# A two-layer graph network in fp32: four batches together through layer 1, its adjacency products in two Strassen levels

## The chip, the cores and the metric

The kernel runs on one core of one Trainium2 chip. The metric is the device time of one execution in microseconds (us), a median over several executions. All data is fp32.

The engines are named as in the profile: PE (TensorE, matmuls), PEld (its weight loads), DVE (VectorE), ACT (ScalarE), POOL (GpSimd), SP (SyncE, which here only issues DMAs). A matmul multiplies a stationary operand of at most 128 by 128 (loaded first) with a moving operand of up to 512 columns, and leaves the result in one of eight PSUM banks, each of 512 fp32 columns over 128 partitions. ACT and DVE bring results from there into SBUF.

## What is computed

The input `x` has 32 batches of 512 nodes by 128 features; `adj` is 512 by 512.

```
# layer 0: x, adj x, adj^2 x, adj^3 x, mixed by weights (adj is given twice, so pairs of weights add up)
y_1 = einsum('bnik,iok->bno', x_all, weight_1)
x = layernorm(x + y_1)
# layer 1: five gated steps on h, starting from h = x
m_in = m_out = einsum('nm,bmd->bnd', adj, h)
u3 = h @ u3_w.T + u3_b
z  = sigmoid(av @ w3_w.T + w3_b + u3)
r  = sigmoid(av @ w4_w.T + w4_b + u3)
hv = tanh(av @ w5_w.T + w5_b + (r * h @ u5_w.T + u5_b))
h  = (1 - z) * h + z * hv
x = layernorm(x + h)
```

Since both halves of `av` are the same m = adj h, each gate weight is the sum of its two halves: one 128 by 128 matrix each (`w3s`, `w4s`, `w5s`).

## The kernel before, in words

**Tiling.** A node is (partition, k) with k from 0 to 3, so an array of one batch is four chunks of 128 by 128. The 32 batches are 16 pairs. `pair(q, key0)` (L1035) takes a pair through `layer0` (L701) and then through five steps. `h` is kept feature-major (`hT`, 128 features by 512 nodes); the adj product needs it node-major (`X`). `turn` (L345) makes one from the other: a DVE transposition of 32 by 32 blocks (L360), four DMAs to a buffer `d` in HBM (L352) and one back (L358).

**The adj product of a step.** `pair_product` (L514) multiplies the pair's two batches, side by side, with adj as a 2 by 2 block product in Winograd's form of Strassen: POOL makes sums of the input blocks (L511) and PE makes 7 half-products for 8, each of two matmuls of 256 columns (L524). `seven` (L393) arranges them for both kinds of product. It uses three banks, `a`, `b` and `c`: products 1, 3, 5 and 6 accumulate one after the other in bank `a`, and between them ACT copies the sum so far (L385), since each intermediate sum is itself wanted; so product 3 must wait for the copy after product 1, and so on. DVE adds what else belongs together (L389).

**The two-level form** exists already for the `adj x` of layer 0: from the third pair on, two pairs (four batches) go through `quad_product` (L565), which splits each block again: 49 quarter products for 64, each one matmul of 128 columns (L628). It is done in two runs of `seven`: half A, whose seven groups hold four quarter products each, and half B, whose seven groups hold three. In B, DVE adds A's result while it takes the product out of PSUM (L386), and further sums are made by DVE (L685).

**The gates of a step**, one batch at a time (`gates`, L901, matmuls of 512 columns in L909): w4·m into bank `pr`, w3·m into `pz`, w5·m plus u5·(r h) into `ph`. u3·h goes into a bank of its own (L1049), ACT moves it to SBUF with its bias (L1054), and DVE adds it to `pr` (L915) and `pz` (L922) ahead of the sigmoids (L917, L924). L918 makes r h, L956 the tanh, L970 and L972 make z (hv - h), and POOL adds that to h (L974).

**Layer 0 after the product**: weights (L766), the product with adj squared (L831), a layer norm (`norm`, L304: moments on DVE, L313 and L314; the power -1/2 and small steps on POOL, L317 to L322; the application on ACT, L330). **The end**: the last pairs' last steps transpose on PE, and the last pair ends in halves (`last_finish`, L977).

**What sets the order.** No queue is filled in program order: `Plan` (L47) is a list scheduler that runs when the program is built. Each operation has an engine, an assumed duration, what it comes after, buffers it takes and gives back (`slots`, L157) and a key; the ready operation with the lowest key goes next on its engine. `KEYS` (L24) and `LONG` (L25) are keys of the pairs and the distance of steps. The order of instructions on each engine is then fixed in the program.

Of the kernel before, what the change touches and what calls it, by code (L numbers as in the profile page):

```python
# [9 lines left out]
F32 = mybir.dt.float32  # L10
# [4 lines left out]
P = 128  # L15
NK = 4
# [6 lines left out]
ON_PE = {14: 2, 15: 2}  # L23
KEYS = [-2.0, 20.0, 50.0, 68.0, 92.0, 118.0, 154.0, 168.0, 186.0, 214.0, 234.0, 268.0, 294.0, 322.0, 346.0, 358.0]  # L24
LONG = 19.0  # L25
# [101 lines left out]
def gnn_resnorm_kernel(  # L127
# [22 lines left out]
    small = ctx.enter_context(tc.tile_pool(name="small", bufs=16))  # L150
# [3 lines left out]
    def tiles(tag, n, shape=(P, N), pool=work):  # L154
# [4 lines left out]
        d=tiles("d", 6, (NR, R, NR, P), dram),  # L159
        hd=tiles("hd", 6, (P, 2, NK, P), dram),  # L160
        xg=tiles("xg", 2, (P, 2, NK, P)),
        xT=tiles("xT", 3),
        M=tiles("M", 1, (P, 4, N)),
        SA=tiles("SA", 1, (P, 25, P)),
        SB=tiles("SB", 1, (P, 15, P)),
        UY=tiles("UY", 2, (P, 4, N)),
        h0=tiles("h0", 4, (P, 2, NK, P)),
        hT=tiles("hT", 8),
        X=tiles("X", 3),
        uT=tiles("uT", 6),  # L170
        rh=tiles("rh", 2),
        z=tiles("z", 3),
        m=tiles("m", 5),
        S=tiles("S", 2, (P, 7, H, P)),
        v=tiles("v", 5),
        two=[None] * 5,
        inside=[None] * 17,
# [9 lines left out]
    mhalf = const.tile([P, 2 * NK], F32, tag="mhalf", name="mhalf")  # L187
# [5 lines left out]
    TT = const.tile([P, 7, 4, P], F32, tag="TT", name="TT")  # L193
    make_identity(nc, ident)
    nc.vector.memset(mhalf, -0.5)

    def load_x(q, b, engine=nc.sync):
        engine.dma_start(plan[f"xg{q}"][:, b], x[2 * q + b].rearrange("(p k) c -> p k c", k=NK))

    def loaded_x(q, key):  # L200

        take = [("xg", f"xg{q}")]
        first = plan("SP", 0.42, lambda: load_x(q, 0), take=take, key=key, late=4.5)
        return first, plan("SP", 0.42, lambda: load_x(q, 1), after=[first], key=key, late=4.5)

    def second_x(after):

        emit = lambda b: load_x(1, b, nc.scalar)
        after = after + [place]
        first = plan("ACT", 0.45, lambda: emit(0), after=after, key=-60.0, late=3.2)  # L210
        return first, plan("ACT", 0.45, lambda: emit(1), after=after, key=-60.0, late=3.2)
# [6 lines left out]
    def first_x():  # L218
        emit = lambda: load_x(0, 0)
        a = plan("SP", 0.42, emit, take=[("xg", "xg0")], key=-99.0, late=2.9)  # L220
        b = plan("SP", 0.42, lambda: load_x(0, 1), key=-98.0, late=3.4)
        return a, b
# [34 lines left out]
    w0_in = plan("SP", 0.45, lambda: nc.sync.dma_start(w_of(), w0), take=[("UY", "w0")], key=-70.0, late=7.0)  # L257
# [10 lines left out]

    w0_ready = plan("DVE", 2.3, layer0_weights, after=[w0_in], give=[("UY", "w0")], key=-40.0)

    place = plan("-", 0.0, lambda: None, take=[("xg", "xg1")], key=-99.0)
# [5 lines left out]
    def gate_weight(src, name):  # L277
        halves = lambda: plan[name][:, : 2 * P].rearrange("p (h o) -> p h o", h=2)
        w = const.tile([P, P], F32, tag=name, name=name)
# [3 lines left out]
        ready.append(plan("DVE", 0.28, emit, after=[got], give=[("z", name)], key=26.0))  # L283
        return w

    def plain(src, name):
        t = const.tile(list(src.shape), F32, tag=name, name=name)
        ready.append(plan("SP", 0.45, lambda: nc.sync.dma_start(t, src), after=[later], key=23.5, late=4.0))
        return t

    w3s, w4s, w5s = (gate_weight(s, n) for s, n in ((w3, "w3s"), (w4, "w4s"), (w5, "w5s")))
    u3s, u5s = plain(u3, "u3s"), plain(u5, "u5s")
    b3s, b4s, b5s = plain(b3, "b3s"), plain(b4, "b4s"), plain(b5, "b5s")
    ub3s, ub5s = plain(ub3, "ub3s"), plain(ub5, "ub5s")
    hv_b = const.tile([P, 1], F32, tag="hv_b", name="hv_b")
    hv_ready = plan("DVE", 0.1, lambda: nc.vector.tensor_tensor(hv_b, b5s, ub5s, ALU.add), after=ready, key=26.0)
    weights = ready + [hv_ready]
# [6 lines left out]
    def norm(n, name, src_of, dst_of, after, give, key, by_dve=False):  # L304
# [11 lines left out]
        def power():  # L316
            nc.gpsimd.tensor_scalar(rstd, mv[:, :, 1], EPS, None, ALU.add)  # L317
            if not by_dve:
                nc.gpsimd.tensor_scalar(shift, mv[:, :, 0], -1.0, None, ALU.mult)
            nc.gpsimd.tensor_tensor(rstd, rstd, mhalf[:, :n], ALU.pow)  # L320
            if not by_dve:
                nc.gpsimd.tensor_tensor(shift, shift, rstd, ALU.mult)  # L322
# [14 lines left out]
        p = plan("POOL", 1.2 if by_dve else 1.75, power, after=got, key=key)  # L337
# [55 lines left out]
    def seven(name, after, us, terms, product, outs, key, shape, take=(), give=()):  # L393
# [19 lines left out]
        c1 = out(first_out, "a", [p1], 0, 0)  # L413
# [17 lines left out]
    an_of = lambda km: plan[f"an{km // H}"].rearrange("p b k c -> p (b k c)").rearrange("p (k n) -> p k n", k=H)  # L431
    an_ready = []
    for km in range(NK):
        emit = lambda km=km: transposes(plan[f"ba{km}"], lambda k: at[:, k, chunk(km)])
        take = [("bank", f"ba{km}")] + ([("h0", f"an{km // H}")] if km % H == 0 else [])
        tr = plan("PE", 0.44, emit, after=at_in, take=take, key=SQ_KEY)
        emit = lambda km=km: nc.scalar.copy(an_of(km)[:, km % H], plan[f"ba{km}"])
# [3 lines left out]
    an_sum = lambda i: lambda: plan[f"anS{i // H}"][:, i % H].rearrange("p k c -> p (k c)").rearrange(  # L441
        "p (k c) -> p k c", k=H
    )
    sums = []
    for i, (a, b, op) in enumerate(
# [8 lines left out]
        take = [("h0", f"anS{i // H}")] if i % H == 0 else []  # L454
# [26 lines left out]
    give = [("h0", f"{t}{i}") for t in ("an", "anS") for i in range(2)]  # L481
# [32 lines left out]
    def pair_product(X_of, turned, name, dst, S, slots, after, key):  # L514
# [21 lines left out]
        F = lambda i: lambda: fit(S(i), turned)  # L536
        if turned:
            f11 = copied(S_of(4), X11, True, "ACT", [own], key)
            f12 = copied(S_of(5), X12, True, "ACT", [f11], key)
        else:  # L540
            f11 = f12 = own
        s0 = add(0.73, F(0), X21, X22, ALU.add, both, key)
        s1 = add(0.73, F(1), F(0), X11, ALU.subtract, [s0], key)
        s2 = add(0.73, F(2), X11, X21, ALU.subtract, both, key)
        s3 = add(0.73, F(3), X12, F(1), ALU.subtract, [s1], key)
        f22 = copied(S_of(6), X22, True, "POOL", both, key) if turned else own
        L = (S_of(4), S_of(5), S_of(6)) if turned else (X11, X12, X22)
        t = lambda i: lambda: T[:, i]
        terms = [
            (L[0], lambda: B11, [f11, in11]),  # L550
            (L[1], lambda: B21, [f12, in21]),
# [3 lines left out]
            (L[2], t(3), [f22, T_sums[3]] + both),  # L555
# [4 lines left out]
            name, [f11], 0.86, terms, product, into(dst, HN), key, half_bank, give=give  # L560
        )
        read = [s0, s1, s2, s3, f11, f12, f22] if turned else p + [s2, s3]
        return [[e11, e12], [e21, e22]], [read] * 2

    def quad_product(X_of, name, after, key):  # L565
# [3 lines left out]

        SA, SB, PA, M = (f"{t}{name}" for t in ("SA", "SB", "PA", "M"))  # L570
        X = lambda i, j, b: lambda: X_of(2 * i + b)[:, j * H : (j + 1) * H]

        LOW, HIGH = slice(3, 5), slice(5, 7)
        part = lambda S, at, w: lambda: plan[S][:, at + w.start : at + w.stop]

        def inner(S, at, a, after):

            out = lambda i: lambda: plan[S][:, at + i]
            s2 = add(0.45, out(1), a(0, 0), a(1, 0), ALU.subtract, after, key)
            s0 = add(0.45, out(3), a(1, 0), a(1, 1), ALU.add, after, key)  # L580
            s1 = add(0.45, out(0), out(3), a(0, 0), ALU.subtract, [s0], key)
            s3 = add(0.45, out(2), a(0, 1), out(0), ALU.subtract, [s1], key)
            return s1, s2, s3, s0

        quarter = lambda i, j: lambda b, k: lambda: X_of(2 * i + b)[:, j * H + k]
        at_of = {0: 4, 1: 11, 2: 18}

        own = plan("-", 0.0, lambda: None, after=[o for a in after for o in a], take=[("SA", SA), ("UY", PA)], key=key)
        s0, s2, s1 = [], [], []
        for b, w in ((0, HIGH), (1, LOW)):  # L590
            s0.append(add(0.73, part(SA, 11, w), X(1, 0, b), X(1, 1, b), ALU.add, [own], key))
            s2.append(add(0.73, part(SA, 4, w), X(0, 0, b), X(1, 0, b), ALU.subtract, [own], key))
            s1.append(add(0.73, part(SA, 18, w), part(SA, 11, w), X(0, 0, b), ALU.subtract, s0[-1:], key))
        x11 = inner(SA, 0, quarter(0, 0), [own])
        q = lambda i: lambda: plan[SA][:, 4:].rearrange("p (o b) c -> p o b c", o=3)[:, :, i]
        ready = s0 + s1 + s2
        i2 = add(0.98, q(1), q(5), q(3), ALU.subtract, ready, key)
        i0 = add(0.98, q(3), q(3), q(4), ALU.add, [i2], key)
        i1 = add(0.98, q(0), q(3), q(5), ALU.subtract, [i0], key)
        i3 = add(0.98, q(2), q(6), q(0), ALU.subtract, [i1], key)  # L600


        def lefts(S, at, direct):
            sums = {2: 0, 4: 1, 6: 2, 3: 3}
            if direct is None:
                sums = {**sums, 5: 4, 0: 5, 1: 6}
# [579 lines left out]
```

## Time and profile before

| what | us |
| --- | --- |
| median of 3 runs (1510.89 to 1514.23) | 1511.45 |
| span of the profiled execution | 1510.3 |
| PE busy | 1493.2 |
| DVE busy | 1024.4 |
| POOL busy | 848.7 |
| ACT busy | 750.7 |
| the granted TensorE clock, mean | 0.997 of full speed |

The span runs from the first to the last instruction of the profiled execution; the median lies 1.15 us above it. Matmul records overlap: one matmul in fp32 leaves two records, and each is drawn longer than the distance from its start to that of the next[...]. So how long PE needs for a matmul is read from the distance of starts in the timeline, not from the mean of a group. "idle before" in a group's row is the engine's idle time just before such instructions, with the one that ended it.

### The profile page before, as it was taken

Reading aid. Unit: us, or ns where it says so; the run is one execution under the profiler, and the core shown is the slowest. Engines: PE = TensorE matmul, PEld = TensorE weight load, DVE = VectorE, ACT = ScalarE, POOL = GpSimd, SP = SyncE. Lnnn points to the kernel's source line nnn. Section 1 sums busy time; section 2 is a strip of 40 time slices with the busy share of each in tenths; the row PEclk is TensorE's granted clock in tenths of the full one; section 3 lists DMA queues with packets and bytes.
Section 4 is the critical chain, followed back from the end, with each engine's and each line's share of the span. In section 5 each row is a group of like instructions: output and inputs, shape, how many; then the busy total and the mean of one; then the engine's idle time right before and its main releaser. Section 6 shows DMA issues by size and latency. Waiting matters only on the chain.

```text
span 1510.3 us, 21064 instructions
## 1 busy us (share of the span) xinstructions
PE 1493.2 (99%) x6562; PEld 1042.3 (69%) x6562; DVE 1024.4 (68%) x2125; ACT 750.7 (50%) x1584; POOL 848.7 (56%) x1207
## 2 busy tenths in 40 slices
PE   8999999999999999999999999999999999999997
PEld 7877777676667776677676766676766776666665
DVE  6566666767776758667767567768477666766665
ACT  3454444654644644455445445546444455545454
POOL 4856834764544947756367455558464644543454
PEclk9999999999999999999999999999999999999998
DMA  3114423333333433334243242534333332433310
GB/s 110 57 56 112 107 75 92 110 107 84 105 103 107 126 98 93 107 95 119 71 139 90 77 120 92 133 98 126 81 109 92 90 84 70 119 86 89 77 50 28
DMA packets 166176, 142.91 MB, mean 95 GB/s; under 512 B 18992, under 2 KB 128048, under 8 KB 166064
## 3 DMA queue, kind: packets, MB, share of 16 engines
q1 hardware_dynamic: 165776, 141.04, 33.9%
q8 instruction: 52, 0.85, 0.3%
q14 instruction: 60, 0.49, 0.1%
q10 hardware_dynamic: 288, 0.52, 0.1%
HBM read 71.76 MB, written 69.73 MB: 94 GB/s over the span
## 4 chain that ended last, share of the span: by engine, by line
PE 94%; DVE 2%; POOL 1%; issue 1%; DMA 1%; SPq 0%; ACT 0%; POOLq 0%; DVEq 0%
PE bank L909 35%; PE bank L524 32%; PE bank L1049 9%; PE bank L766 6%; PE bank L831 6%; PE bank L628 4%; PE bank L460 1%; PE bank L302 0%; POOL rstd L320 0%; POOL S L511 0%; DVE M L685 0%; DMA at<-in_adjT 0%; DVE UY L685 0%; PE bank L1018 0%; DMA X<-d 0%
## 5 line engine op out<-in xcount | busy, mean ns | idle before, releaser
L974 POOL TENSOR_TENSOR hT<-z,hT 128x512 f32<-128x512 f32 x156 | 199.0, 1281 | 303.9 <-DVE z L972 297.9
L524 PE MATMUL bank<-T,S 128*128 128x256 f32 x1232 | 307.0, 379 | 0.2 <-POOL S L511 0.2
L524 PEld LDWEIGHTS bank<-T,S 128*128 128x128 f32 x1232 | 229.1, 190 | 78.2 <-ACT m L385 28.9
L385 ACT COPY m<-bank 128x256 f32<-128x256 f32 x320 | 119.1, 372 | 277.6 <-PE bank L524 276.5
L524 PE MATMUL bank<-at,S 128*128 128x256 f32 x824 | 211.4, 379 | 0.9 <-ACT S L504 0.6
L389 DVE TENSOR_TENSOR m<-bank,m 128x256 f32<-128x256 f32 x240 | 100.3, 419 | 137.0 <-PE bank L524 94.7
L524 PEld LDWEIGHTS bank<-at,S 128*128 128x128 f32 x824 | 153.7, 190 | 57.3 <-issue 37.3
L970 DVE TENSOR_TENSOR bank<-bank,hT 128x512 f32<-128x512 f32 x156 | 107.8, 694 | 104.4 <-ACT bank L956 103.6
L909 PE MATMUL bank<-rh,u5s 128*128 128x512 f32 (+1 forms) x324 | 159.3, 587 | 0.2 <-ACT bank L936 0.2
L1049 PE MATMUL bank<-hT,u3s 128*128 128x512 f32 x320 | 159.3, 592 | 0.0
L909 PE MATMUL bank<-m,w4s 128*128 128x512 f32 x320 | 158.6, 592 | 0.0
L909 PE MATMUL bank<-m,w3s 128*128 128x512 f32 x320 | 157.0, 592 | 0.0
L909 PE MATMUL bank<-m,w5s 128*128 128x512 f32 x320 | 155.1, 593 | 0.2 <-DVE M L389 0.2
L917 ACT ACTIVATE bank<-bank 128x512 f32<-128x512 f32 x160 | 93.2, 583 | 121.1 <-DVE bank L915 120.7
L1054 ACT ACTIVATE uT<-bank,ub3s 128x512 f32<-128x512 f32 x160 | 109.7, 687 | 83.9 <-PE bank L1049 82.7
L915 DVE SCALAR_TENSOR_TENSOR bank<-bank,b4s,uT 128x512 f32<-128x512 f32 x160 | 119.6, 750 | 46.3 <-PE bank L909 44.1
L956 ACT ACTIVATE bank<-bank,hv_b 128x512 f32<-128x512 f32 x158 | 104.3, 662 | 77.1 <-PE bank L909 76.0
L922 DVE SCALAR_TENSOR_TENSOR bank<-bank,b3s,uT 128x512 f32<-128x512 f32 x160 | 118.9, 750 | 13.8 <-PE bank L909 13.1
L924 ACT ACTIVATE z<-bank 128x512 f32<-128x512 f32 x160 | 95.1, 595 | 59.9 <-DVE bank L922 55.7
L360 DVE STREAM_TRANSPOSE v<-hT 128x512 f32<-128x512 f32 x152 | 105.5, 699 | 20.0 <-POOL hT L974 19.4
L918 DVE TENSOR_TENSOR rh<-bank,hT 128x512 f32<-128x512 f32 x160 | 107.8, 679 | 10.0 <-ACT bank L917 9.2
L972 DVE TENSOR_TENSOR z<-bank,z 128x512 f32<-128x512 f32 x156 | 105.1, 682 | 1.6
(182 smaller groups left out, 2456.1 us busy)
## 6 DMA issues: line engine op xcount, KB each, us to landing
d<-v SPq DMA_DIRECT2D x832, 64.0 KB, 1.8
X<-d SPq DMA_DIRECT2D x152, 256.0 KB, 2.8
v<-d SPq DMA_DIRECT2D x56, 256.0 KB, 2.8
xg<-in_x SPq DMA_DIRECT2D x30, 256.0 KB, 3.0
out<-h SPq DMA_DIRECT2D x30, 256.0 KB, 2.1
hd<-h SPq DMA_DIRECT2D x13, 512.0 KB, 3.8
h<-hd SPq DMA_DIRECT2D x13, 512.0 KB, 3.9
at<-in_adjT SPq DMA_DIRECT2D x4, 256.0 KB, 5.3
```

Source lines behind the costliest of these rows:

```text
L360: blocks = lambda: nc.vector.transpose(plan[f"v{name}"], src_of())
L385: return "ACT", COPY[cols], lambda src: nc.scalar.copy(dst(i, j), src)
L524: nc.tensor.matmul(dst, lhsT=left[:, k, :], rhs=right[:, k, :], start=(first and k == 0), stop=(last and k == H - 1), skip_group_check=True,)
L909: nc.tensor.matmul(plan[dst][:, c], lhsT=w, rhs=plan[src][:, c], start=first, stop=last, skip_group_check=True)
L915: emit = lambda: nc.vector.scalar_tensor_tensor(plan[pr], plan[pr], b4s, plan[uT], ALU.add, ALU.add)
L918: emit = lambda: nc.vector.tensor_tensor(plan[rh], plan[pr], plan[h], ALU.mult)
L922: emit = lambda: nc.vector.scalar_tensor_tensor(plan[pz], plan[pz], b3s, plan[uT], ALU.add, ALU.add)
L970: emit = lambda: nc.vector.tensor_tensor(plan[ph], plan[ph], plan[h], ALU.subtract)
L972: emit = lambda: nc.vector.tensor_tensor(plan[z], plan[ph], plan[z], ALU.mult)
L974: emit = lambda: nc.gpsimd.tensor_tensor(plan[h], plan[z], plan[h], ALU.add)
L1049: emit = lambda bn=bn, hb=h[b]: nc.tensor.matmul(plan[bn], lhsT=u3s, rhs=plan[hb], start=True, stop=True)
L1054: emit = lambda bn=bn, uT=uT: nc.scalar.activation(plan[uT], plan[bn], AF.Identity, bias=ub3s)
```

## The change

Layer 1 takes quads of four batches instead of pairs; `quad(Q, key0)` replaces `pair`, and 8 quads replace 16 pairs.

1. `quad_product` serves the steps too, except those that `PAIRS = {0: (0, 1), 6: (3, 4), 7: (3, 4)}` names (quad: steps), where the new `pair_products` makes two pair products as before. Its input sums are laid out anew (blocks in `SA` and `SB` side by side, so that the inner sums take all blocks at once), copies of plain blocks are made by ACT, and half B adds onto the result of half A in place, all of its seven takings-out on DVE. Of the further sums, three are on DVE and two on POOL.
2. `gates`: u3·h goes straight into `pr`, under w4·m; after the sigmoid of r has read the bank, (w3 - w4)·m is added in the same bank, which makes it the sum for z. So the bank for u3·h, its ACT move and both DVE additions go. m now lies in two pieces of 256 columns, so each of its products is two matmuls. The last addition of h moves from POOL to DVE.
3. `norm`: two of POOL's small steps move to DVE, one goes.
4. Buffers are shared: `E` (5 tiles for four batches each) holds inputs, U and Y, h0, X; `Q` (2) holds m and the layer-0 product; `SB` is one, `SA` two. Every quad's h0 is written to HBM and fetched again at the end. Weights lie in the part of `at` that isn't read any more.
5. The last step of the last quad ends on PE (`finish`), the special endings in halves are gone. All keys are new.

```diff
-ON_PE = {14: 2, 15: 2}
-KEYS = [-2.0, 20.0, 50.0, 68.0, 92.0, 118.0, 154.0, ...]
-LONG = 19.0
+KEYS = [-11.9, 27.7, 78.0, 130.0, 180.1, 230.1, 270.6, 308.3]
+PAIRS = {0: (0, 1), 6: (3, 4), 7: (3, 4)}
+ON_PE = {7: 1}
+LONG = 29.5
...
-        M=tiles("M", 1, (P, 4, N)),
-        SA=tiles("SA", 1, (P, 25, P)),
-        SB=tiles("SB", 1, (P, 15, P)),
+        E=tiles("E", 5, (P, 4, N)),
+        Q=tiles("Q", 2, (P, 5, N)),
+        SA=tiles("SA", 2, (P, 29, P)),
+        SB=tiles("SB", 1, (P, 21, P)),
...
+    emit = lambda: nc.vector.tensor_tensor(w3s, w3s, w4s, ALU.subtract)
...
         def power():
-            nc.gpsimd.tensor_scalar(rstd, mv[:, :, 1], EPS, None, ALU.add)
             nc.gpsimd.tensor_tensor(rstd, rstd, mhalf[:, :n], ALU.pow)
+        def shifts():
+            nc.vector.scalar_tensor_tensor(shift, mv[:, :, 0], -1.0, rstd, ALU.mult, ALU.mult)
...
+    def quad_product(X_of, turned, name, after, key):
+        for b in range(2):
+            f11[b] = copy(blk(SA, 0, b), X(0, 0, b), lo)
+            s0[b] = outer(blk(SA, 2, b), X(1, 0, b), X(1, 1, b), ALU.add, hi)
+            s1[b] = outer(blk(SA, 3, b), blk(SA, 2, b), X(0, 0, b), ALU.subtract, ...)
+            s2[b] = outer(blk(SA, 1, b), X(0, 0, b), X(1, 0, b), ALU.subtract, ...)
+            f12[b] = copy(blk(SB, 0, b), X(0, 1, b), [ownB, *lo])
+            f22[b] = copy(blk(SB, 1, b), X(1, 1, b), [ownB, *hi])
+            s3[b] = outer(blk(SB, 2, b), X(0, 1, b), blk(SA, 3, b), ALU.subtract, ...)
...
+        inA = inner(SA, 1.28, f11 + s0 + s1 + s2)
+        inB = inner(SB, 1.0, f12 + f22 + s3)
...
+        u = sum_of("DVE", 0.8, M_of(3), M_of(3), M_of(0), ends)
+        v = sum_of("POOL", 1.28, M_of(4), M_of(1), M_of(2), ends)
+        e22 = sum_of("POOL", 1.28, M_of(4), M_of(4), M_of(3), [u, v])
...
-            into(dstB, 3 * P, plus),
+            into(dstB, 3 * P, dstB),
+            out_after=[u, v],
...
+        e21 = sum_of("DVE", 0.8, M_of(1), M_of(1), M_of(3), [u] + endsB)
+        e12 = sum_of("DVE", 0.8, M_of(2), M_of(2), M_of(3), [u] + endsB)
...
+    def gates(name, m, h, after, h_in, early, key):
+        emit = lambda: mm(pr, u3s, h, True, False)
+        p = plan("PE", 0.86, emit, after=early + h_in + weights, take=[("bank", pr)], key=key - 0.01)
+        emit = lambda: mm_m(pr, w4s, False, False)
+        p = plan("PE", 0.86, emit, after=after + [p], take=[("bank", ph)], key=key)
+        r = act(ph, pr, AF.Sigmoid, r_b, 0.59, key, [p], take=[("rh", rh)])
+        r2 = dve(rh, ph, h, ALU.mult, key, [r])
+        p2 = plan("PE", 0.86, lambda: mm_m(pr, w3s, False, True), after=[r], key=key + 0.5)
+        zs = act(z, pr, AF.Sigmoid, z_b, 0.59, key + 0.5, [p2], take=[("z", z)], give=[("bank", pr)])
+        p3 = plan("PE", 1.73, candidate, after=[p2, r2], give=[("rh", rh)], key=key + 0.8)
+        t = act(ph, ph, AF.Tanh, hv_b, 0.66, key + 0.8, [p3])
+        t = dve(ph, ph, h, ALU.subtract, key + 0.8, [t])
+        t = dve(ph, ph, z, ALU.mult, key + 0.8, [t, zs], [("z", z)])
+        return p3, dve(h, ph, h, ALU.add, key + 0.8, [t], [("bank", ph)])
...
+    for Q in range(NP // 2):
+        quad(Q, KEYS[Q])
```

In the changed kernel the lines are L662 (quarter products), L747 (pair products of the steps), L1010 and L1014 (gates), L865 and L930 (layer 0), L420 (ACT copies out of PSUM), L421 and L424 (DVE takings-out), L699 (further sums), L602 and L544 (POOL sums), L606 (ACT copies of blocks).

## The prediction

> **What bounds the kernel now.** I read the page's busy times first, then its slices and the chain that ended last, then PE's starts in the timeline, then the windows of the two ends.
>
> ```profile
> PE 1493.2 (99%) x6562; PEld 1042.3 (69%) x6562; DVE 1024.4 (68%) x2125; ACT 750.7 (50%) x1584; POOL 848.7 (56%) x1207
> ...
> PE   8999999999999999999999999999999999999997
> ...
> PE 94%; DVE 2%; POOL 1%; issue 1%; DMA 1%; SPq 0%; ACT 0%; POOLq 0%; DVEq 0%
> ```
>
> PE is busy in 1493.2 of 1510.3 us, full in all slices but the ends, and is 94% of the chain. A busy PE need not be at its peak, so I read the distance of starts (columns: start, length, engine, line, operation, records):
>
> ```profile
> 699.87 1.05 PE L831 MATMUL bank<-S,at 128*128 128x128 f32 x8
> 700.76 1.06 PE L831 MATMUL bank<-UY,at2S 128*128 128x128 f32 x8
> ...
> 706.82 1.89 PE L524 MATMUL bank<-T,S 128*128 128x256 f32 x8
> 708.55 1.02 PE L909 MATMUL bank<-rh,u5s 128*128 128x512 f32 x2
> ...
> 713.71 1.88 PE L909 MATMUL bank<-m,w4s 128*128 128x512 f32 x4
> 715.43 1.88 PE L909 MATMUL bank<-m,w3s 128*128 128x512 f32 x4
> ```
>
> Eight records of 128 columns take 0.89 us, eight of 256 take 1.73, four of 512 take 1.72. At two records each, a matmul costs **0.2225, 0.4325 and 0.86 us**: close to proportional to its columns, 4% dearer per column at 128. The program has 1335, 1180 and 798 of them: 297.0 + 510.4 + 686.3 = 1493.7 us, PE's busy time to 0.5. So the kernel before is PE's columns plus 16.6 us, and these lie at the ends (columns: window, its length, busy us of PE, PEld, DVE, ACT, POOL):
>
> ```profile
> 0.00:10.00 10.00, 5.29 (x16) 4.27 (x17) 0.76 (x2) 2.83 (x4) 3.52 (x10) 1.00 0.62 203
> ...
> 1490.00:1500.00 10.00, 8.83 (x36) 5.16 (x34) 7.37 (x17) 6.79 (x16) 2.01 (x2) 1.00 0.11 44
> 1500.00:1511.00 11.00, 1.90 (x8) 1.45 (x8) 3.73 (x16) 1.51 (x4) 4.86 (x9) 0.59 0.16 56
> ```
>
> 4.7 us are lost at the start and 10.3 at the end. In between, nobody keeps PE waiting: its groups away from the ends show 1 us of idle time at most, while the others wait for it or for each other:
>
> ```profile
> POOL hT L974 <- DVE z L972: 297.9, 97, 18.7
> ACT m L385 <- PE bank L524: 276.5, 266, 5.8
> ```
>
> **What the Trainium skill says.** "TensorE: Matmul & The Clock Gate", part 2, gives N/2.4 + 2.5 ns as the distance of matmuls of N columns, and 55.6 ns measured at 128. A record here is 111 ns at 128 columns and 430 at 512: twice that gap (111 and 432); the trace agrees. "SBUF — State Buffer", "two separate sides": a DVE operation with two SBUF inputs and a GpSimd operation exclude each other for a whole instruction. The trace agrees: L685, both inputs in SBUF, takes 669 ns at best, 744 in the median, 1755 at worst. "PSUM — Partial Sum Buffer", "The four PSUM rules": POOL can't touch PSUM, and a partial sum may be read within an accumulation group. The first is why h's last addition, now from a bank, must be DVE's; `seven` already does the second before.
>
> **The change, part by part.** Counts are from the order of the changed program, which is built but has not run.
>
> *Adj products.* L524's 1148 matmuls of 256 columns become 28 (L557) and 168 (L747): 952 × 0.4325 = 411.7 us less. Quarter products go from 343 to 2009 = 41 × 49 (34 steps, 7 layer-0 products; so the change does what it says): 1666 × 0.2225 = 370.7 more. A quad step costs 49 × 0.2225 = 10.9 us where two pair products cost 28 × 0.4325 = 12.1. **Minus 41.0 us** of PE, on the path.
>
> *Gates.* Still five products for each of 160 batch-steps, but the 480 with m are now two halves: 480 × (0.865 - 0.86) = **plus 2.4**. Sixteen fewer transpositions on PE: **minus 3.6**. The whole: 2985 × 0.2225 + 1184 × 0.4325 + 320 × 0.86 = 664.2 + 512.1 + 275.2 = **1451.5 us, 42.2 less**.
>
> *Other engines*, off the path so long as PE is fed. DVE: out go L915 and L922 (238.5) and 204 of L389 (× 0.419 = 85); in come 160 additions of h × 0.69 = 110, takings-out of quad products 164 × 0.55 + 123 × 0.55 + 123 × 0.685 = 242 less 41 before, 88 more sums of L685's kind at 0.74 to 1.1 = 65 to 97, small norm steps 13: near **1110 us, 75%**. POOL: out go L974 and its like (206), 208 pair sums × 0.74 (154), 50 copies (20), small norm steps (42), the old quad sums (113); in come 328 × 0.74 = 243, 41 × 9.5 = 390 (two of 1.28, six of 1.005, two of 0.46) and 82 × 1.28 = 105: near **1050, 71%**. ACT: minus L1054 (110), minus 272 copies × 0.372 (101), plus 80 and 59 for larger copies: near 680. None passes PE.
>
> *New waits of PE.* In `seven`, product 3 waits for the copy after 1, 5 for that after 3, 6 for that after 5. From the timeline, ACT starts about 0.20 us after PE's next slot, and I add 0.10 for the way back: 0.89 us with a 512-column copy (0.587), 0.67 with a 256-column one (0.372), 0.85 with DVE's 0.55. I laid the matmul costs along the order and measured what PE has to do in between. Half A, 123 such gaps: 5 of zero, 8 of 0.44, 20 of 0.7 to 0.86, falling short by 8.5 us together. B: 0.8 (one of zero, 29 just wide enough). Weights of layer 0: 2.0; pair products: 1.3; from w4 to (w3 - w4), behind the sigmoid: 0.8. Sum **13 us**; the same count before gives about 1. Queued behind the waiting matmul is all of PE. The bound below is zero (a stall in one place widens the next gap), above it twice the sum, when DVE is late.
>
> *Queues and DMA.* From the last candidate of a quad to its next product PE has at least 25 us of other work, in place of the 12 or so of tanh, three DVE operations, transposition, four writes and a fetch: hidden. SP issues 1201 DMAs for 1148, also off the path. Only the last step is tight: 10.3 us for about 12: **plus 2**. At the start the transpositions of the first h0 come 4.4 us of PE work after the product that their norm needs; moments of eight chunks (8 × 0.45), 1.3 for the power and three ACT steps of 0.49 make about 7.5: **plus 3**. After the last matmul group of the gates: tanh 0.66, three DVE steps 2.1, PE 0.9, moments 1.7, power 1.3, four applications 1.4, storing 3.2, and gaps: 12.0 for the 13.5 of before: **minus 1.5**.
>
> *B's first taking-out* waits for u (DVE) and v (POOL), and with it B's third product: after A's last product 0.2, a DVE operation of 0.69, v at 1.28, the taking-out at 0.55 and the ways between, 3.1 us. PE's work in between is 2.0 to 14.5 us; five of 41 places fall short, by 2.4 together. If v stands behind another POOL sum of 1.28 each time, 12.6. I take **4**.
>
> Sum: 1451.5 + 16.6 + 13 + 2 + 3 - 1.5 + 4 = 1488.6 of span; the median stood 1.15 above its span: **1490 us**. What is late next: DVE's queue.
>
> **The rivals.**
> - *As here*, PE bound with 10 to 31 us of new waits: 1479 to 1500, chance 0.62.
> - *PE filled as before.* The order was planned with durations near the measured ones, and before it left no waits. Then 1451.5 + 16.6 + 1 = 1469 (1464 to 1478). Against it: eleven places where dependent products stand back to back. 0.14.
> - *The waits eat more*: 1500 to 1508.4, 0.07, and all of it to within 0.2%, 0.05.
> - *Slower: DVE takes over half B.* All seven takings-out of B are DVE's, where ACT took the first kind before; they queue behind four batches' gates (in a quad step DVE works about 4 × 3.5 for these and 8.6 for the product, of 28 us of PE) and behind sums that POOL's lock can hold to 1.75. 29 of B's gaps are one matmul wide (0.86), so one other DVE operation of 0.69 ahead of each stops PE. It decides from 42.2 / 41 = 1.03 us a quad product; at 1.5 us: 1468 + 62 = 1530. For it: DVE from 68 to 75%. Against: POOL and ACT, at 50 to 56%, cost PE nothing before, and a late PE gives DVE time to catch up. 0.12.
>
> **How the numbers follow.** A measurement of this kernel can tell about 0.2% from no change. Faster by more: 0.62 + 0.14 + 0.07 = 0.83; within: 0.05; slower: 0.12. The range 1468 to 1510 leaves out the better part of the second case and the slower one, about 0.2.
>
> **What would show it.** PE's busy time near 1452 to 1470 with about 8,900 records (two for each of 4489 matmuls); idle before L662 by ACT's and DVE's takings-out of some 10 us, near none before L1010 and L1014; DVE near 75%, POOL near 70%; sums of L699 at 0.75 to 1.1 us. I am wrong if matmuls of 128 columns stand further apart than 0.1115 us in L662 (at 0.12, 1666 × 0.017 = 28 us), if PE's idle is over 60 us, or if it waits for DVE before L662 and L1014.

## The result, and the profile after

The changed kernel takes **1529.29 us** (median of 4 runs, 1525.06 to 1531.43) beside 1511.69 for the kernel before (median of 4; the 1511.45 above is of three of them): ratio 1.0114, interval 1.0101 to 1.0126. It is slower by 1.1%. The forecast was 1490 (1468 to 1510), faster. The profiled execution has a span of 1528.9 us.

Busy times, PE's slices and the chain that ended last, from the page of the changed kernel:

```profile
PE 1478.9 (97%) x8930; PEld 1239.8 (81%) x8930; DVE 1156.8 (76%) x2322; ACT 698.7 (46%) x1424; POOL 1027.5 (67%) x1178
...
PE   8899899899999999999999999999999999999997
...
PE 44%; DVE 5%; DMA 2%; issue 1%; SPq 1%; POOL 1%; ACT 0%; POOLq 0%; DVEq 0%; ACTq 0%
```

PE's share of the span fell from 99 to 97%, and its busy time by 14 us only, though its columns are some 42 us less. The shares of the chain add up to 55% only: it could be followed back to 685.9 us and no further. Of the 840 us that it covers, PE has 81%, where it had 94% of nearly the whole span before; DVE has 9 and DMA 3%. Part of PE's waiting hides in "busy", as PE's timeline shows:

```profile
702.94 1.05 PE L662 MATMUL bank<-TT,SA 128*128 128x128 f32 x8
703.83 1.03 PE L1014 MATMUL bank<-Q,at 128*128 128x256 f32 x4
704.70 1.13 PE L662 MATMUL bank<-TT,SA 128*128 128x128 f32 x8
705.66 1.03 PE L1014 MATMUL bank<-Q,at 128*128 128x256 f32 x4
```

Eight records of L662 take 0.89 us the first time (703.83 - 702.94), 0.96 the second, and neither line notes idle time: a record is drawn 277 ns long while the next should start after 111, so a start that comes up to 165 ns late leaves no gap. I therefore measure against the columns: span less columns was 1510.3 - 1493.7 = 16.6 us, and is now 1528.9 - 1451.5 = **77.4 us**. From the distances of starts (records of 128, 256 and 512 columns set at 111, 216 and 430 ns), 154 starts came 60 to 165 ns late (15.1 us together; before 26, 2.7 us), 29 came 165 to 400 ns late (8.5), 40 came 400 to 1000 ns late (26.8) and 8 more than that (17.2). Not all of this is waiting: 43 of the 154 (4.4 us) lie where the granted clock is 0.5 (last section), so there the records themselves are slow.

The ends, in the windows of the engines (window, its length, busy us of PE, PEld, DVE, ACT and POOL, then the granted clock, the DMA share and GB/s):

```profile
0.00:10.00 10.00, 6.23 (x29) 5.33 (x30) 2.37 (x6) 3.41 (x5) 3.52 (x10) 1.00 0.63 208
...
1510.00:1520.00 10.00, 9.19 (x60) 7.73 (x59) 8.26 (x29) 5.21 (x12) 2.44 (x3) 1.00 0.14 53
1520.00:1529.00 9.00, 1.16 (x8) 0.97 (x8) 4.65 (x24) 3.01 (x8) 2.43 (x3) 0.63 0.23 87
```

They lose 3.8 and 8.6 us where they lost 4.7 and 9.5 (the 10.3 of the forecast counts 0.7 us behind the end of the span): the loss is in between. The groups that answer to those of the forecast (busy us, mean ns, then the idle time before and what ended it):

```profile
L1014 PE MATMUL bank<-Q,at 128*128 128x256 f32 x1920 | 476.7, 381 | 10.8 <-DVE rh L1024 6.2 <-DVE Q L699 4.2 <-ACT bank L1028 0.4
L662 PE MATMUL bank<-TT,SA 128*128 128x128 f32 x1312 | 171.5, 277 | 5.5 <-ACT Q L420 5.5
L699 DVE TENSOR_TENSOR Q<-Q 128x512 f32<-128x512 f32 x123 | 138.7, 1153 | 3.9 <-ACT Q L420 0.8 <-DVE Q L424 0.5
L662 PE MATMUL bank<-TT,SB 128*128 128x128 f32 x984 | 135.5, 278 | 7.5 <-DVE Q L421 7.4
L699 POOL TENSOR_TENSOR Q<-Q 128x512 f32<-128x512 f32 x82 | 114.2, 1393 | 94.2 <-DVE Q L424 67.2 <-DMA d<-v 16.2 <-ACT SA L606 4.7
...
L353 DVE SCALAR_TENSOR_TENSOR shift<-mv,rstd 128x4 f32<-128x4 f32 x63 | 26.5, 422 | 5.5 <-POOL rstd L350 5.3
L368 DVE TENSOR_SCALAR rstd<-mv 128x4 f32<-128x4 f32 x64 | 19.7, 316 | 0.0
```

PE waits in the gates (L1014) for DVE, where the forecast had next to nothing, and in half B (TT,SB) for DVE. DVE's quad sums take 1153 ns in the mean; 40 of the 123 take under 700, ten some 1750, three 3.2 to 7.3 us. Of the 81 that take over 760, 78 end after one POOL operation has ended, and in 70 of these POOL's next one is held up in its turn; the other three wait through 3, 4 and 9 of them. The longest, in the timeline of all engines:

```profile
273.54 6.58 POOL L544 TENSOR_TENSOR SA<-SA 128x384 f32<-128x384 f32 x8
...
274.58 0.66 ACT L1028 ACTIVATE bank<-bank,r_b 128x512 f32<-128x512 f32 x1 [1.92 <-issue]
274.74 7.90 DVE L699 TENSOR_TENSOR Q<-Q 128x512 f32<-128x512 f32 x2
...
280.09 1.39 POOL L602 TENSOR_TENSOR SB<-E,SA 128x256 f32<-128x256 f32 x2
282.56 0.68 DVE L1024 TENSOR_TENSOR hT<-bank,hT 128x512 f32<-128x512 f32 x1
283.16 0.68 DVE L1024 TENSOR_TENSOR rh<-bank,hT 128x512 f32<-128x512 f32 x1
...
283.89 1.65 PE L1014 MATMUL bank<-Q,at 128*128 128x256 f32 x3 [5.10 <-DVE rh L1024]
```

The first of the two DVE sums starts at 274.74 and ends at 282.04. All that time POOL runs one SBUF operation after the other, the last to 281.48; the sum ends 0.56 us after that. Behind it, after the second sum and one more DVE operation, stands r x h, whose sigmoid (274.58 and 0.66 us more) was ready at 275.24, and behind r x h stands PE: 5.10 us idle, its longest wait in the kernel.

### The profile page after: what moved, and what is told of

Read it like the earlier page. It is cut to its first block, busy times and chain, and to the rows that moved or that the text cites. A ratio compares the mean times of both kernels' runs of the same rounds, so it can differ in the third digit from the quotient of the medians.

```text
span 1528.9 us, 26035 instructions
## 1 busy us (share of the span) xinstructions
PE 1478.9 (97%) x8930; PEld 1239.8 (81%) x8930; DVE 1156.8 (76%) x2322; ACT 698.7 (46%) x1424; POOL 1027.5 (67%) x1178
## 3 DMA queue, kind: packets, MB, share of 16 engines
q8 instruction: 70, 1.15, 0.3%
## 4 chain that ended last, share of the span: by engine, by line
PE 44%; DVE 5%; DMA 2%; issue 1%; SPq 1%; POOL 1%; ACT 0%; POOLq 0%; DVEq 0%; ACTq 0%
PE bank L1014 15%; PE bank L662 14%; PE bank L1010 9%; PE bank L747 3%; PE bank L930 2%; PE bank L865 2%; DVE bank L1024 1%; SPq L387 1%; DVE Q L699 1%; DMA d<-v 1%; DMA E<-d 1%; DVE st L346 1%; DVE mv L347 0%; DVE v L395 0%; DVE hT L1024 0%
## 5 line engine op out<-in xcount | busy, mean ns | idle before, releaser
L1014 PE MATMUL bank<-Q,at 128*128 128x256 f32 x1920 | 476.7, 381 | 10.8 <-DVE rh L1024 6.2
L1014 PEld LDWEIGHTS bank<-Q,at 128*128 128x128 f32 x1920 | 348.2, 191 | 107.3 <-issue 50.5
L544 POOL TENSOR_TENSOR SB<-SB 128x384 f32<-128x384 f32 x164 | 168.2, 1026 | 100.2 <-ACT SB L606 94.3
L544 POOL TENSOR_TENSOR SA<-SA 128x128 f32<-128x128 f32 (+2 forms) x246 | 228.9, 946 | 6.9
L424 DVE TENSOR_TENSOR Q<-bank,Q 128x512 f32<-128x512 f32 (+2 forms) x282 | 165.9, 592 | 74.2 <-PE bank L662 33.9
L420 ACT COPY Q<-bank 128x512 f32<-128x512 f32 (+1 forms) x212 | 113.5, 536 | 214.7 <-PE bank L662 173.4
L662 PEld LDWEIGHTS bank<-TT,SA 128*128 128x128 f32 x1312 | 160.5, 192 | 21.2 <-issue 11.8
L699 POOL TENSOR_TENSOR Q<-Q 128x512 f32<-128x512 f32 x82 | 114.2, 1393 | 94.2 <-DVE Q L424 67.2
L662 PE MATMUL bank<-TT,SA 128*128 128x128 f32 x1312 | 171.5, 277 | 5.5 <-ACT Q L420 5.5
L1010 PE MATMUL bank<-rh,u5s 128*128 128x512 f32 x320 | 163.9, 594 | 0.0
L1010 PE MATMUL bank<-hT,at 128*128 128x512 f32 x320 | 159.3, 593 | 0.0
L602 POOL TENSOR_TENSOR SA<-E 128x256 f32<-128x256 f32 x164 | 122.5, 760 | 53.1 <-DMA E<-d 26.2
L662 PEld LDWEIGHTS bank<-TT,SB 128*128 128x128 f32 x984 | 124.3, 191 | 38.3 <-DVE Q L421 21.5
L662 PE MATMUL bank<-TT,SB 128*128 128x128 f32 x984 | 135.5, 278 | 7.5 <-DVE Q L421 7.4
L699 DVE TENSOR_TENSOR Q<-Q 128x512 f32<-128x512 f32 x123 | 138.7, 1153 | 3.9 <-ACT Q L420 0.8
L421 DVE TENSOR_TENSOR Q<-bank,Q 128x384 f32<-128x384 f32 x164 | 90.0, 549 | 55.9 <-PE bank L662 40.4
```

What stands on the lines that cost most here:

```text
L420: return "ACT", COPY[cols], lambda src: nc.scalar.copy(dst(i, j), src)
L421: return "DVE", ADD[cols], lambda src: nc.vector.tensor_tensor(dst(i, j), src, plus(i, j), ALU.add)
L424: return "DVE", ADD[cols], lambda src: nc.vector.tensor_tensor(dst(i, j), src, dst(i, j), ALU.add)
L544: emit = lambda: nc.gpsimd.tensor_tensor(dst(), a(), b(), op)
L602: emit = lambda: nc.gpsimd.tensor_tensor(fit(d(), turned), A(), B(), op)
L662: nc.tensor.matmul(dst[:, o], lhsT=L[i](), rhs=R_of(i), start=(first and o == 0), stop=last, skip_group_check=True,)
```

## The experiments

Three theories. **1**: DVE and POOL exclude each other on operations with two SBUF inputs; the three DVE sums of a quad product are held up, and DVE is late for the gates and half B. **2**: the order, with four batches in step and few shared buffers, leaves PE too little other work, whatever a sum takes. **3**: the dependent products of half A, back to back behind ACT's copies. Differences are of medians, with the ratio to the kernel before and its interval; the kernel before, run again with each group of experiments, took 1511.20 to 1511.49.

### The sums cut to 32 columns

```
-            emit = lambda: by.tensor_tensor(d(), a(), b(), ALU.add)
+            emit = lambda c=slice(0, R if engine == "DVE" else N): by.tensor_tensor(d()[:, c], a()[:, c], b()[:, c], ALU.add)
```

> The changed kernel with the three quad sums that DVE adds (u, e21, e12 in L699) cut to 32 of 512 columns; the sums of the other columns are left out, the order on every engine is the same. The changed kernel took 1529.3 us. Theory 1, DVE is late because these sums take 1.15 us under POOL's lock instead of 0.7: most of PE's 28 us of waiting for DVE goes, 1500 to 1510. Theory 2, the waits lie in the order and in the few shared buffers, and DVE's sums are one duration among many: 1518 to 1525, with PE still idle before L662, L1014 and the layer-0 products. Theory 3, ACT's takings-out between dependent products: 1526 to 1529.

Measured: 1511.29 us, ratio 0.9995 (0.9983 to 1.0006): **18 us less** than the changed kernel. Between the bands of theories 1 and 2, nearer to the first. But DVE's group shows that the sum's width was not what it paid for:

```profile
L699 DVE TENSOR_TENSOR Q<-Q 128x32 f32<-128x32 f32 x123 | 62.4, 533 | 0.0
```

A sixteenth of the columns still takes 533 ns in the mean, and one of these took 6.27 us, at 271.3. So this run didn't take the exclusion away.

### Without the small norm steps

```
-            nc.vector.scalar_tensor_tensor(shift, mv[:, :, 0], -1.0, rstd, ALU.mult, ALU.mult)
+            pass
...
-        emit = lambda: nc.vector.tensor_scalar(rstd, mv[:, :, 1], EPS, None, ALU.add)
+        emit = lambda: None
```

> The changed kernel without the two small DVE steps of each norm (L353 and L368, 422 and 316 ns; the small constant and the shift are left out of the normalisation), otherwise in the same order. If these steps, which were moved from POOL and queue on DVE, are what makes DVE late: 1515 or less. Theories 1, 2 and 3: 46 us of DVE's work at places where PE waits for other things, 1524 to 1529.

Measured: 1519.0, ratio 1.0060 (1.0044 to 1.0077): 10 us less, between all expectations. DVE did 40 us less (1116.8 busy), and a quarter of that came through. It says that DVE's lateness costs, not yet why DVE is late. But these steps are themselves held by POOL in the changed kernel: wherever no POOL operation overlaps them they take at most 170 ns, and each of the 52 that took over 250 (of 127) ended 16 to 30 ns after the end of a POOL operation. That is some 26 of their 46 us.

### Both cuts

The two edits above together.

> The changed kernel with both cuts: DVE's three quad sums on 32 of 512 columns and the two small norm steps left out (those parts of the computation are left out), same order. The single cuts gave 1511.3 and 1519.0 against 1529.3: 18 and 10 us. If both shorten one thing, DVE's queue, and each microsecond of it counts: about 1501. If there is a floor under them, waits that DVE's load doesn't set: 1506 to 1511, with PE idle before L662 by ACT's copies, before L865 and before L747 as in the single cuts.

Measured: 1508.69, ratio 0.9982 (0.9971 to 0.9992): on the floor that was the second expectation, and 3 us less than the cut sums alone. The two don't add: with the sums nearly gone, the norm steps cost little. It is not each microsecond of DVE that counts.

### The sums without two SBUF inputs

```
-            emit = lambda: by.tensor_tensor(d(), a(), b(), ALU.add)
+            emit = lambda: by.transpose(d(), b()) if engine == "DVE" else by.tensor_tensor(d(), a(), b(), ALU.add)
```

> The changed kernel with DVE's three quad sums replaced by a transposition of the same 128x512 tile (one SBUF input; L395 has it at 0.70 us), so the sums are left out and DVE's queue keeps an operation of the length that an undisturbed sum has. If it is the mutual exclusion with POOL that costs (1.15 for 0.70 us, and POOL's own operations held up): most of the 18 us go, 1511 to 1516. If it is DVE's time as such, 0.45 of 1.05 us are saved: 18 x 0.43 = 8 us, 1521.

Measured: **1505.69**, ratio 0.9965 (0.9952 to 0.9978): **23.6 us less** than the changed kernel, with full-width operations in the same order, and 5.6 us less than with sums of 32 columns. The busy times of this run, and its groups:

```profile
PE 1470.5 (98%) x8930; PEld 1238.7 (82%) x8930; DVE 1100.7 (73%) x2322; ACT 698.9 (46%) x1424; POOL 986.9 (66%) x1178
```

```profile
L1014 PE MATMUL bank<-Q,at 128*128 128x256 f32 x1920 | 473.7, 380 | 0.7 <-ACT bank L1028 0.4 <-DVE rh L1024 0.2
L699 POOL TENSOR_TENSOR Q<-Q 128x512 f32<-128x512 f32 x82 | 104.3, 1272 | 98.8 <-DVE Q L424 78.7 <-DMA d<-v 9.3 <-ACT E L420 4.1
L662 PE MATMUL bank<-TT,SB 128*128 128x128 f32 x984 | 134.4, 277 | 3.6 <-DVE Q L421 3.4
L699 DVE STREAM_TRANSPOSE Q<-Q 128x512 f32<-128x512 f32 x123 | 82.1, 692 | 3.9 <-ACT Q L420 0.8 <-DVE Q L424 0.5
```

The operation takes 692 ns and never over 714. The wait in the gates is gone (10.8 to 0.7 us), that of half B halved, and POOL's operations are shorter too (1393 to 1272 ns; 41 us of POOL in all). DVE works 20 us longer here than with the narrow sums, and the kernel is faster: theory 1, and the exclusion rather than DVE's load. Only the sums are freed: the small norm steps are still held by POOL in this run (404 and 306 ns in the mean, 118 and 135 at best). It gains more than either expectation had, since these took the run with narrow sums for one without exclusion.

### ACT's copies in half A cut

```
+        w = 4 if name < "1" or name[0] == "x" else 1
+        dst1 = lambda i, j: plan[M][:, :w, block(i, j)]
...
-            into(dst, N),
+            (into(dst1, N)[0], into(dst, N)[1]),
```

(with the copy's source cut alike.)

> The changed kernel with ACT's takings-out of half A cut from four blocks to one in 31 of 41 quad products (three quarters of what they take out is left out there), same order: the copy falls from 0.58 to about 0.30 us. Theory 3, products 3, 5 and 6 that stand close behind their copies: the 9.3 us of waiting for ACT's copy mostly go, and what hangs on them, 1515 to 1521. If these waits only stand in for others (a later wait takes the time up): 1524 to 1529.

Measured: 1531.67, ratio 1.0127 (1.0095 to 1.0159): above both bands, no gain in the median; the four runs spread from 1522.86 to 1535.11, so a gain of 3 to 4 us can't be excluded. In the profiled run, the fastest of them, the cut copies take 265 ns and PE's wait for the copies fell from 5.5 to 3.1 us, but its wait for DVE in half B is 9.3 us for 7.4. Theory 3's wait is real and small, and seems to stand in for others.

### Pair products in all steps, and the gates alone

```
-PAIRS = {0: (0, 1), 6: (3, 4), 7: (3, 4)}
+PAIRS = {Q: (0, 1, 2, 3, 4) for Q in range(8)}
```

> The changed kernel with pair products in all 40 steps in place of 34 quad products: four batches together, the same gates, the same buffers. PE's columns grow by 34 x 1.21 = 41 us, to 1492.6; without waits that is 1510. If the waits are the quad products' (theory 1, or theory 3), about as many as before the change remain: 1512 to 1525. If they come from four batches in step and from buffers shared between them (theory 2), the waits stay near 45 to 60 us: 1545 to 1565.

Measured: 1543.89, ratio 1.0211 (1.0194 to 1.0228), 14.6 us more than the changed kernel for 41 us more columns, and just under the band of theory 2. Span less columns is 1540.1 - 1492.6 = 47.5 us, 31 more than before the change, without one quad sum in a step. PE's own list of waits in this run:

```profile
PE bank L747 <- ACT SA L763: 9.7, 10, 2.1
PE bank L1014 <- ACT bank L1028: 4.7, 5, 2.0
...
PE bank L930 <- DVE v L421: 3.0, 2, 2.6
```

(us in total, times, longest.) Others are late here: ACT's copies of the inputs. So four batches going together can cost some 30 us of waiting without quad products. That theory 2 has this share in the changed kernel too isn't shown: the keys, searched for quad products, were kept, and a step of pair products is longer.

The gates in the kernel before, in short (with u3's product in `pr`, `w3d` = w3 - w4 and the biases in the sigmoids, as in the changed kernel):

```
+        emit = lambda: mm(pr, w4s, m, False, False)
...
+        r = act(ph, pr, AF.Sigmoid, r_b, 0.59, key, [p], take=[("rh", rh)])
+        r2 = dve(rh, ph, h, ALU.mult, key, [r])
+        p2 = plan("PE", 0.86, lambda: mm(pr, w3d, m, False, True), after=[r], key=key + 0.5)
```

> The kernel before with the new gates alone (r and z from one bank, u3's product added in it, the biases in the sigmoids, h's last addition on DVE), but for the last step of the last two pairs, which keeps the old ones. PE's columns stay at 1493.7. If the wait behind the sigmoid and for r x h (L1014, 16.7 us in the changed kernel) belongs to the gates: 1520 to 1530. If it belongs to the order around them: 1510 to 1517.

Measured: 1518.19, ratio 1.0036 (1.0023 to 1.0049): 6.7 us more than the kernel before, between the two bands and nearer to the second. In this run none of PE's groups in the new gates shows idle time, and starts there are 0.6 us late in all; the waits are elsewhere and spread (the longest but for the first load are 2.2 us for POOL's sums and 2.2 in the last pairs' end; starts of the layer-0 weights are 6.2 us late for 2.0). The new dependence of w3 - w4 on the sigmoid costs next to nothing by itself; why the other waits grew stays open.

### The order made again, and a sum without exclusion

The first of these gives the planner durations as measured, new keys and a shift for each step:

```
+        ("DVE", 0.42): (0.341, 0.2), ("DVE", 0.48): (0.4, 0.2), ("DVE", 0.1): (0.32, 0.2),
...
+        us, late = self.US.get((engine, us), (us, self.LATE[engine])) if late is None else (us, late)
...
+            key = key0 + FROM + LONG * s + NUDGE.get(8 * s + Q, 0.0)
```

The second also moves u into a PSUM bank, so that each DVE sum reads one input from PSUM:

```
+        emit = lambda: nc.scalar.copy(U(), M_of(0)())
+        u = plan("ACT", 0.6, emit, after=ends, take=[("bank", ub)], key=key + AT_SUM)
+        u = sum_of("DVE", 0.69, U, M_of(3), U, [u])
...
+        e22 = sum_of("DVE", 0.69, M_of(4), M_of(4), U, [u, v])
...
+        e21 = sum_of("DVE", 0.69, M_of(1), M_of(1), U, [u] + endsB)
+        e12 = sum_of("DVE", 0.69, M_of(2), M_of(2), U, [u] + endsB)
```

> The changed kernel with its order made again: the planner is given durations as the traces show them (DVE's quad sum 1.12 us, takings-out and gate operations at their pace back to back), and the start keys are searched anew, with a shift of its own for each step; 26 quad and 14 pair steps instead of 34 and 6, so PE's columns are 8 x 1.21 = 9.7 us more. The sums stay as they are. If the 36 us of other new waits (1505.7 of the unlocked run against 1469) are the order's: 1500 to 1512. If the exclusion between DVE and POOL, which no planned duration describes, decides in any order: 1515 to 1530.

Measured: 1519.31, ratio 1.0048 (1.0034 to 1.0063): in the band of the exclusion, yet 10 us less than the changed kernel with 9.7 us more columns. One sum took 10.0 us in this run. The order helps, and alone doesn't win.

> u of the quad product lies in a PSUM bank: ACT copies M0 there, DVE adds M3, and e21, e12 and e22 are DVE additions with one input in PSUM (e22 moves from POOL to DVE), so that no quad sum of DVE has two SBUF inputs. Keys searched anew as in the run before, 31 quad steps (columns 3.6 us more than the changed kernel's). If the exclusion (24 us) and the order (some 30 us) are the two causes of the loss: 1492 to 1502, faster than the kernel before. If the bank that u holds makes PE wait: 1505 or more.

Measured: **1499.66**, ratio **0.9918** (0.9902 to 0.9935), as expected: faster than the kernel before and than the changed one. DVE's sums e12, e21 and e22 in it (three for each of 38 quad products), and PE's group in the gates:

```profile
L1028 PE MATMUL bank<-Q,at 128*128 128x256 f32 x1920 | 473.8, 380 | 1.9 <-ACT bank L1042 1.5 <-DVE rh L1038 0.4
...
L708 DVE TENSOR_TENSOR Q<-Q,bank 128x512 f32<-128x512 f32 x114 | 74.4, 677 | 4.0 <-POOL Q L708 2.1
```

The exclusion put back into it:

```
-        e12 = sum_of("DVE", 0.69, M_of(2), M_of(2), U, [u] + endsB)
+        e12 = sum_of("DVE", 0.69, M_of(2), M_of(2), M_of(3), [u] + endsB)
```

(e21 and e22 likewise.)

> The run before in the same order, but e21, e12 and e22 take M3 from SBUF where they took u from PSUM (so u is left out of them): three DVE sums with two SBUF inputs in each quad product, as in the changed kernel. If the exclusion costs some 20 us in any order: 1512 to 1525. If it only hurt in the old order, where DVE was already late: within 5 us of the run before.

Measured: 1523.45, ratio 1.0078 (1.0062 to 1.0093): **23.8 us more** than the run before it, every instruction in the same place on its engine, one operand of 114 additions in SBUF instead of PSUM:

```profile
L1028 PE MATMUL bank<-Q,at 128*128 128x256 f32 x1920 | 475.2, 381 | 12.5 <-DVE rh L1038 9.7 <-ACT bank L1042 1.5 <-DVE Q L708 1.2
...
L708 DVE TENSOR_TENSOR Q<-Q 128x512 f32<-128x512 f32 x114 | 113.1, 1016 | 3.1 <-POOL Q L708 2.6
```

The same two lines, 677 against 1016 ns, and 1.9 against 12.5 us of PE. Removed from the sums in the old order, put back in a new one, the exclusion costs 23.6 and 23.8 us.

And the edit of u alone, in the changed kernel with its keys and durations:

> u in PSUM as in e9, with the keys and the planned durations of the changed kernel, so the planner lays out another order that nobody has looked at. If taking away the exclusion is enough by itself: 1500 to 1508, as in the run with the transpositions. If the order matters as much: 1515 to 1530.

Measured: 1526.40, ratio 1.0097 (1.0079 to 1.0116). With no sum held, but in the order that the old keys happen to give the altered program, PE waits elsewhere: 26.7 us more than the same edit with keys searched for and measured durations, which has three more pair steps. So the order is the second half of the matter. It is also 20.7 us more than the run with transpositions, but that run has neither the bank that u holds nor ACT's copy into it; how much of the 20.7 these two cost, no run separates.

## Why the prediction was wrong, point by point

**The columns: right to some 2 us.** The forecast had 1451.5 us, 42.2 less, and some 8,900 records; there are 8930. The middle distance of starts in L662 is 0.1117 us, 0.0002 over the bound that I had set, worth 2 to 3 us over 5970 records. (That a record of an fp32 matmul takes twice the gap quoted there is read from this trace alone; the quoted figure doesn't say it.) The transpositions on PE, 64 before and 48 after, were priced wrongly: each leaves one record, not two, and the next starts 0.11 us later, not 0.2225 (four of them take 0.44 us, at 8.11 in the changed kernel). So the columns are about 7.3 us fewer before and 5.5 fewer after, the change saves 40.4, and that their sum met PE's busy time to 0.5 was luck.

**New waits, "sum 13 us", and B's first taking-out, 4: the step that failed.** With 2, 3 and -1.5 for last step, start and end, the forecast added 20.5 us to the 16.6 of before. The profiled run has 77.4 - 16.6 = **60.8** (1.8 of them the price of the transpositions). Of these, 25.7 (1528.9 - 1503.2, the spans of the changed kernel and of the run with the sums freed) are DVE's three sums and POOL in each other's way. The sum of waits counted distances in PE's order against fixed durations; a duration that depends on what POOL does at that moment had no place in it. "Sums of L685's kind at 0.74 to 1.1" were priced as DVE's busy time, off the path; the 1.755 worst case stood in the text and was used only for a rival. The mean became 1.153, not far above that price: what failed is that the extra time was taken to be off the path. The largest single piece, 5.1 us of PE's idle time, hangs on one sum of 7.3 us; the rest is spread.

**"Near none before L1010 and L1014": wrong.** 10.8 us idle before L1014, 10.4 of them for DVE; 0.7 with the sums freed. PE waiting for DVE before L662 and L1014 was one of the forecast's own signs of being wrong. The wait stands where I had counted 0.8, because r x h queues behind the sums on DVE, which is the question the forecast should have put to each new DVE operation: who is behind it?

**Half A, 8.5: right in size; half B, 0.8 + 4: only with the sums freed.** The late starts behind ACT's copy of L420 sum up to 8.1 us, those behind DVE's L421 to 9.6 in the changed kernel and 4.8 with the sums freed. Cutting A's copies gained nothing, though: by the two waits in that run, what is saved on ACT is spent on DVE.

**The other 35.1 us, for which the forecast had 20.5.** In the run with the sums freed PE's idle time, by windows, is:

| window, us | before | changed | sums freed |
| --- | --- | --- | --- |
| 0 to 80 | 5.5 | 8.6 | 8.8 |
| 80 to 200 | 0.6 | 5.2 | 3.5 |
| 200 to 1440 | 1.5 | 24.1 | 8.7 |
| 1440 to the end | 9.5 | 12.2 | 11.8 |

The start (+3.3 for 3) is right by luck: PE's wait for the norm ahead of the first h0's transpositions is 0.5 us, and 2.6 of the 3.3 are one wait of L930 for DVE's taking-out (L421). The end (+2.3 for 0.5) is nearly 2 us short. Not forecast are 2.9 us in 80 to 200, the layer-0 weights at 7 us of late starts (L865; 2.0 in the forecast), the product with adj squared at some 4 (L930, the wait of 2.6 among them; none), and what no idle time shows: starts 60 to 165 ns late, 10.8 us of all this (3.2 of them at the halved clock) against 2.7 before. No experiment separates these smaller waits further, and their cause stays open. That the order sets them is shown only as far as another order of nearly the same products moved the time by some 27 us.

**Other engines.** POOL 1027.5 for 1050, ACT 698.7 for 680. DVE 1156.8 for 1110: the two small norm steps, booked at 13 us, are 46.2, more than half of it a wait for POOL, and without them the kernel is 10 us faster. Without the quad sums they cost about 3, so they matter on a DVE that is late.

**The rivals.** The slower one, 1530, has the time, in part by luck: its ground (DVE late, sums that POOL holds up) is what happened, its place is not. It saw half B's takings-out stopped by other DVE operations, at 1.5 us a quad product. Of PE's waits for DVE, more stood in the gates than in half B (10.4 and 7.4 us), and B's fell to 3.4 by freeing the sums alone. I gave it 0.12 for want of a price on the exclusion. "PE filled as before" rested on durations "near the measured ones": the planner has 0.8 us for a sum of 1.15 and 0.1 for norm steps of 0.32 and 0.42.

## What to carry to other kernels

Price an operation whose length depends on another engine by its long cases and by who queues behind it, not by its mean alone: 123 sums whose extra length adds up to 57 us on an engine 76% busy cost 24 us of PE. On a DVE that shares the time with a busy POOL, give an addition one PSUM input (here an ACT copy and one bank per product) rather than two SBUF inputs. And when a change moves the balance of a planned kernel, plan again with measured durations before judging it: the same idea took 1526 and 1500 us in two orders.

## What the runs showed of the hardware

The Trainium skill ("SBUF — State Buffer", "SBUF: two separate sides") says that the operation that starts first has the shared ports for the whole of its instruction and the other blocks. The traces agree and show more: a DVE sum that waits mostly gets its turn after one POOL instruction (78 of 81 in the changed kernel), but not always. In the timeline above a sum waits through POOL's row of nine until POOL pauses, 7.3 us; others took 6.3 (the run with exclusion put back) and 10.0 us (the order made again). What decides between the two isn't shown. The sum's width hardly matters to the wait: 32 columns take 170 ns at best, but 533 in the mean and up to 6.27 us.

Two SBUF inputs aren't the whole condition either. The norm step of L368 reads one SBUF tensor (128x4), and 22 of its 64 took over 250 ns, up to 989, each ending 24 to 30 ns after a POOL operation; at best it takes 135. Transpositions with one SBUF input (692 ns, never over 714) and additions with one input in PSUM (677) weren't held.

After some waits PE runs slower for a while. A window of the changed kernel (columns as above), and PE's timeline at the first long wait in it:

```profile
40.00:80.00 40.00, 35.43 (x255) 33.59 (x254) 23.04 (x67) 12.01 (x28) 27.53 (x32) 0.91 0.14 43
```

```profile
51.96 2.05 PE L930 MATMUL bank<-S,at2S 128*128 128x128 f32 x8 [2.60 <-DVE v L421]
53.80 0.63 PE L662 MATMUL bank<-at,SA 128*128 128x128 f32 x2
54.23 1.49 PE L662 MATMUL bank<-T,SA 128*128 128x128 f32 x6
```

Eight records of 128 columns take 53.80 - 51.96 = 1.84 us, 0.23 each instead of 0.111, and the granted clock of the window is 0.91; in the kernel before, the same window has 1.00. Away from the end, the changed kernel has three stretches at a granted clock of 0.5, 51.3 to 58.1, 177.6 to 181.0 and 283.4 to 286.8 us, during or just after waits of 2.60, of 1.80 and 0.65, and of 5.10 us; after the wait of 2.18 us at 469.14 the clock stays at 1.00. "TensorE: Matmul & The Clock Gate", "Part 1: The HAM clock gate", has an array that falls to half rate after an idle stretch of about 3.4 us; the trace agrees on the half rate, but shorter waits were enough here. The records in the three stretches take some 6 us longer than at full clock, so a wait can cost more than its idle time.
